# Router logits out of the shared expert's rest product, with the rests moved ahead of the router's choice and attention's statistics moved five half slots

## The chip, the core and the metric

The kernel runs on one core of one Trainium2 chip. The core has five engines with a queue each: TensorE (PE; its weight loads are shown as PEld), VectorE (DVE), ScalarE (ACT), GpSimd (POOL) and SyncE (SP, which here only issues DMAs). The metric is device time in microseconds (us): the median of three runs. Lower is better.

## What is computed

The reference is one cross-attention layer and one mixture-of-experts layer on 64 batches of 128 tokens with 128 features, all in float32. Cut to what matters:

```python
x = x + attention(layernorm(x), ctx)        # 16 heads of 64, 77 keys of 96 features per batch
x2 = layernorm(x)
logits = x2 @ router_w.T                    # 8 experts
scores = softmax(logits)
_, idx = top_k(scores, 2)                   # the two best experts of each token
rw = take_along_axis(logits, idx)           # weights are the logits themselves
moe = sum over e: gate[e] * (silu(x2 @ w1[e].T) * (x2 @ w3[e].T)) @ w2[e].T
shared = (silu(x2 @ sw1.T) * (x2 @ sw3.T)) @ sw2.T
x = x + moe + shared                        # inner width of each expert: 176
```

## The kernel before

**Groups, units and half slots.** Four batches make a group, and there are 16 groups (NG). A unit is one batch and 8 of its 16 heads, so a group has 8 units and the kernel 128. The main loop (L1099 to L1116) goes through the units. For unit k it emits, in this order: the scores of unit k + 2 (`scores`, L357), at every second unit the output product of the batch before (`out`, L439), the plan's steps of half slot 2k, the transposes of unit k's weights (`transposes`, L424), the exponentials of unit k + 2 (`exps`, L378), a value product (`values`, L401), the plan's steps of half slot 2k + 1, and the softmax weights of unit k + 2 (`weights`, L382). Everything else hangs in a plan (`at`, L858): a list of steps for each half slot. Group g starts at half slot p = 16 g.

**Order.** The last lines (L1121 to L1131) chain the instructions of each engine in the order in which they were emitted. So an engine works through its queue strictly as written, and a wait of one instruction holds all those behind it on that engine. Buffers are waited for by semaphores.

**Attention.** The query weights are folded into the keys' weights and the output weights into the values' weights. In each half slot PE makes keys for two heads (`keys`, pk, L348) and ACT copies them out (kx, L355). `scores` makes two products into the tile ps, which has one buffer of two PSUM banks (pool ps_s, L92 and L362); DVE takes the maximum (mx, L374) and subtracts it (sc, L376), and then ps is free for the next unit. ACT takes the exponential with the layer norm's factor rs as its scale (L380). DVE sums and inverts (sm, L387; ri, L389), and POOL multiplies (at, L395 to L399). PE transposes (pa, L434), ACT copies (aT, L437). Value products go from pv (L417) to vo by two ACT copies (L422). `out` sums ten products (py, L444), and DVE adds the residual (x1, L445). Six more PSUM banks (pool ps_g, `bank`, L234) serve all the rest. In odd groups four products of the last keys are added (`values_of_last`, pn L454, vn L462), each with an ACT copy and a DMA that ACT issues.

**Layer norm.** `Norm.stats` (L287) is four bn_stats, four bn_aggr and one addition on DVE and one power on POOL. Attention needs only its factor rs, in `exps`; its mean is folded away. The statistics for group g + 1 are taken in half slot p + 2 (L911). For the router, `scale` (L299) makes the normed tokens (pay, four ACT instructions), `transposed` (L313) makes x2T.

**Routing.** The router of group g runs while group g + 1 is in attention, p being that group's first half slot: statistics in p, normed in p + 1, transposed in p + 3, logits in p + 4, the first choice in p + 5, the second in p + 6 (L933 to L935). `logits` (L550) multiplies x2T by the router's weights rw_sb, batch by batch, into the tile pl; DVE copies it (lg, L557), takes the maximum (gm, L559) and subtracts it (gsc, L561), ACT takes the exponential (L562). `choose` (L574) sums (gs, L578), inverts, multiplies, clears what is too small, and finds the first maximum in five instructions (L564). `place` (p + 8) computes each token's row, and `send` (p + 9 to p + 12) scatters the tokens to DRAM, eight DMAs that POOL issues.

**Shared expert.** The inner width of 176 is split into 128 and a rest of 48 (IR). The weights lie packed in wsh_sb: columns 0 to 127 for w1, 128 to 255 for w3, then 112 columns (HI) for both rests, w1's in the first 48 and w3's in the last 48, with 16 columns between them left at zero. `shared_up` (p + 11) multiplies by the first two parts, `shared_rest` (p + 12) by the 112 columns (ph_s, L654), with tanh on ACT (ar_s, L518) and two instructions on DVE (ur_s, L520; hr, L521), `shared_down` (p + 14) by the second weights. The tile hr is one of NHR = 2 that are zeroed once and shared with the experts' blocks. The last three groups (LATE) run the shared expert in the ending.

**Experts.** Tokens are gathered in three sets of 9, 5 and 2 groups. When a set is full, blocks of its tokens go through the experts four at a time (`Quad`): from half slot 160, the start of group 10, the first set's 20 quads run beside attention, the others mostly in the ending (L1043), after attention. A quad loads tokens (xb), copies weights (w, on ACT and DVE), transposes (pt, xT L777), multiplies (p and ph, L782), and sends answers.

Of the kernel before, what the change touches and what calls it, by code (L numbers as in the profile page):

```python
# [27 lines left out]
IR = I - 128  # L28
HI = 64 + IR

W1, W3, WR, W2F, W2R, WALL = 0, 128, 256, 256 + HI, 384 + HI, 512 + HI
G = 4
NG = B // G

# [19 lines left out]

AHEAD = 2
NAT = 2
NHR = 2
NX1 = 3

# [7 lines left out]
def xattn_moe_kernel(  # L67
# [9 lines left out]
    wvT: bass.AP,  # L77
    w_out: bass.AP,
    b_out: bass.AP,
    rwT: bass.AP,  # L80
    wx: bass.AP,
    wsh: bass.AP,
    out: bass.AP,
# [69 lines left out]
    rw_sb = const.tile([D, E], F32, name="rw_sb")  # L153
    wsh_sb = const.tile([128, WALL], F32, name="wsh_sb")

    wx_sb = const.tile([128, E, WALL], F32, name="wx_sb")
    nc.scalar.dma_start(out=bo_sb, in_=b_out.rearrange("(o d) -> o d", o=1).broadcast_to([128, D]))
    nc.sync.dma_start(out=rw_sb, in_=rwT)
    nc.sync.dma_start(out=wsh_sb, in_=wsh)

    def load_expert(e):
# [28 lines left out]

    dest = const.tile([128, 2 * G], F32, name="dest")

    hrs = [const.tile([128, T], F32, name=f"hr_{i}") for i in range(NHR)]

    nobody = const.tile([128, DW], F32, name="nobody")

# [84 lines left out]
    class Norm:  # L281
# [3 lines left out]
            self.name, self.src = name, src  # L285

        def stats(self):  # L287
            st = small.tile([128, G, 6], F32, tag="st", name=f"st_{self.name}")
            self.mv = small.tile([128, G, 2], F32, tag="mv", name=f"mv_{self.name}")
# [4 lines left out]
            ve = small.tile([128, G], F32, tag="ve", name=f"ve_{self.name}")  # L294
            nc.vector.tensor_scalar(ve, self.mv[:, :, 1], EPS, None, ALU.add)
            self.rs = small.tile([128, G], F32, tag="rs", name=f"rs_{self.name}")
            nc.gpsimd.tensor_tensor(self.rs, ve, mhalf, ALU.pow)

        def scale(self, to):  # L299
# [186 lines left out]
    def gated(name, up, silu=False, n=T):  # L486

        p1 = bank(f"p1_{name}")
        up(p1, W1, 128)
        p3 = bank(f"p3_{name}")  # L490
        up(p3, W3, 128)
        a = ffn.tile([128, T], F32, tag="a", name=f"a_{name}")
        h = ffn.tile([128, T], F32, tag="h", name=f"h_{name}", bufs=3)
        of = slice(0, n)
        if silu:
            nc.scalar.activation(a[:, of], p1[:, of], AF.Silu)
            nc.vector.scalar_tensor_tensor(h[:, of], a[:, of], 2.0, p3[:, of], ALU.mult, ALU.mult)
# [8 lines left out]
    def gated_rest(name, up, silu=False, n=T):  # L506
# [4 lines left out]
        hr = hrs[hr_no[0] % NHR]  # L511
        hr_no[0] += 1
        of = slice(0, n)
        if silu:
            nc.scalar.activation(a[64:HI, of], pr[:IR, of], AF.Silu)
            nc.vector.scalar_tensor_tensor(hr[:IR, of], a[64:HI, of], 2.0, pr[64:HI, of], ALU.mult, ALU.mult)
        else:
            nc.scalar.activation(a[:IR, of], pr[:IR, of], AF.Tanh, scale=0.5)  # L518
            u = ffn.tile([128, T], F32, tag="u", name=f"ur_{name}")
            nc.vector.scalar_tensor_tensor(u[64:HI, of], a[:IR, of], 1.0, pr[:IR, of], ALU.add, ALU.mult)  # L520
            nc.vector.tensor_tensor(hr[:IR, of], u[64:HI, of], pr[64:HI, of], ALU.mult)  # L521
        return hr

    class Router:
# [23 lines left out]
            nc.scalar.copy(self.pay[:, 1, :, :D], self.pay[:, 0, :, :D])  # L548

        def logits(self):  # L550
            pl = bank(f"pl_{self.g}")
            for b in range(G):
                nc.tensor.matmul(
                    pl[:, b * E : (b + 1) * E], self.x2T[:, b * NQ : (b + 1) * NQ], rw_sb, start=True, stop=True
                )
            self.lg = lg = self.t3("lg")
            nc.vector.tensor_copy(lg.rearrange("p b e -> p (b e)"), pl[:, : G * E])  # L557
# [4 lines left out]
            nc.scalar.activation(sc, sc, AF.Exp)  # L562
# [32 lines left out]
        def place(self):  # L595
# [20 lines left out]
            )  # L616
            pos = small.tile([128, 2 * G], F32, tag="pos", name=f"pos_{g}", bufs=1)
            for src, to, by in ((at, pos, 1.0), (self.lg, self.pay[:, :, :, D + 1].rearrange("p c b -> p c b"), 0.5)):
                m = small.tile([128, 2, G, E], F32, tag="picked", name=f"picked_{g}", bufs=2)
                for k in range(2):  # L620
                    nc.vector.scalar_tensor_tensor(m[:, k], oh[:, k], by, src, ALU.mult, ALU.mult)
                if to is pos:
                    nc.vector.tensor_reduce(pos, m.rearrange("p c b e -> p (c b) e"), AX.X, ALU.add)
                else:
                    nc.vector.tensor_reduce(to, m, AX.X, ALU.add)
# [31 lines left out]
            self.h = gated(f"s{self.g}", self.up, silu)  # L657

        def shared_rest(self, silu=False):
            self.hr = gated_rest(f"s{self.g}", self.up, silu)  # L660

        def shared_down(self):
            py = bank(f"pf_{self.g}")
# [238 lines left out]
    for g in range(NG):  # L902
# [29 lines left out]
    assert g == NG  # L932
    for g in range(NG - 1):  # L933
        p = 16 * (g + 1)
        routing(g, p, (0, "stats"), (1, "normed"), (3, "transpose"), (4, "logits"), (5, "choose"), (6, "choose_second"))  # L935
    for st in sets:
        for g in range(st.start, min(st.start + st.n, NG - 1)):
            p = 16 * (g + 1)
            routing(g, p, (8, "place"))
            if g < NG - LATE:  # L940
                routing(g, p, (11, "shared_up"), (12, "shared_rest"), (14, "shared_down"), (17, "park"))
            for k in range(4):
                for c in range(2):
                    at(p + 9 + k, lambda g=g, c=c, b=k: routers[g].send(c, b))
# [189 lines left out]
def _laid_out(inputs):  # L1134
# [6 lines left out]
    def packed(w1, w3, w2):  # L1141
# [16 lines left out]
    def by_pair(w):  # L1158
# [15 lines left out]
        "rwT": a["L0_ffn_router_w"].T,  # L1174
        "wx": np.concatenate([packed(w1[e], w3[e], w2[e]) for e in range(E)]),
        "wsh": packed(a["L0_ffn_sw1"], a["L0_ffn_sw3"], a["L0_ffn_sw2"]),
    }


# [17 lines left out]
```

## Time and profile before

| what | us |
|---|---|
| median of three runs (lowest, highest) | 988.45 (987.61, 989.02) |
| the profiled execution | 985.48 |
| its span, first to last instruction | 983.8 |
| PE busy | 924.1 |
| DVE busy | 671.4 |
| ACT busy | 652.8 |
| POOL busy | 517.4 |
| mean granted TensorE clock | 0.978 of full |

The span has four stages. Until about 60 us the first group runs, after the weights are folded. From 60 to 466 us attention and routing of groups 1 to 9 run, without expert blocks. From 466 to about 830 us attention runs with the first set's quads beside it. The rest is the ending.

How to read the views: a row of the order of time shows start, length, engine, line, operation, the tile written and the tiles read; in brackets stands the idle time before it and what ended that. The chain of waits runs back from the last instruction, at each step to what released it. In a row of windows PEclk is the clock that TensorE was granted, 1.00 being full. A PE product's length includes its latency, so products overlap; the chain shows what each adds.

A float32 product takes two passes of weight load and matmul on PE, a transpose takes one: 640 transposes of L434 show 640 rows, 64 logits products of L553 show 128.

### The profile page before, as it was taken

The page shows a single profiled execution, that of the slowest core. Times are in us where ns is not written, and L with a number is a line of the kernel's source. Part 1 is how long each engine was busy: PE and PEld are TensorE (multiplying, and loading weights), DVE is VectorE, ACT ScalarE, POOL GpSimd, SP SyncE. Part 2 cuts the span into 40 slices and gives each one's busy share as a digit, 9 for nine tenths or more (in the row PEclk, how much of TensorE's full clock was granted, in tenths as well). Part 3 has the DMA queues.
Part 4 walks back from the last instruction along what each step waited for, and adds up shares of the span by engine and source line. Part 5 has one row for each costly group of instructions (what it writes and reads, how often), then busy time and mean ns, then how long its engine had stood idle before and what let it go on. Part 6 is the DMA issues. An engine that isn't in the chain of part 4 may idle for free.

```text
span 983.8 us, 18867 instructions
## 1 busy us (share of the span) xinstructions
PE 924.1 (94%) x6123; PEld 771.5 (78%) x6123; DVE 671.4 (68%) x1751; ACT 652.8 (66%) x1420; POOL 517.4 (53%) x688
## 2 busy tenths in 40 slices
PE   8999999999999999999999999999999987779990
PEld 7887877787787878777888788888888876678980
DVE  4566776676667767768687677776676779566642
ACT  5776767676767667675776767667767665556760
POOL 3244563636364544636367375574474564437673
PEclk9999999999999999999999999999999999879996
DMA  6222212212222222122322221223121135723475
GB/s 179 70 62 71 67 41 81 68 57 71 72 71 65 75 73 65 44 86 80 89 70 76 83 82 55 59 69 99 57 85 49 37 121 169 228 66 98 109 212 174
DMA packets 80882, 85.76 MB, mean 87 GB/s; under 512 B 11328, under 2 KB 62912, under 8 KB 80784
## 3 DMA queue, kind: packets, MB, share of 16 engines
q1 hardware_dynamic: 65920, 56.09, 20.8%
q0 software_dynamic: 8864, 18.30, 5.6%
q10 hardware_dynamic: 6000, 10.16, 2.9%
q8 instruction: 49, 0.80, 0.3%
q14 instruction: 49, 0.40, 0.1%
HBM read 48.18 MB, written 36.33 MB: 86 GB/s over the span
## 4 chain that ended last, share of the span: by engine, by line
PE 69%; DVE 10%; ACT 9%; DMA 5%; issue 4%; SPq 2%; POOL 1%; ACTq 0%; DVEq 0%; POOLq 0%
PE py L444 13%; PE ps L365 11%; PE pk L348 11%; PE pv L417 8%; PE pa L434 5%; PE p L782 4%; PE p_s L654 3%; PE pn L454 2%; PE ph L782 2%; PE pq L794 2%; PE pq L795 2%; DMA answers<-y,to 2%; PE pf L667 1%; PE pf L666 1%; DMA out_dram<-yx 1%
## 5 line engine op out<-in xcount | busy, mean ns | idle before, releaser
L348 PEld LDWEIGHTS pk<-cT,wkq_sb 96*128 96x128 f32 x1024 | 157.8, 189 | 70.0 <-issue 42.8
L805 POOL DMA_INDIRECT answers<-y,to x149 | 146.4, 983 | 89.7 <-issue 44.7
L355 ACT COPY kx<-pk 128x308 f32<-128x308 f32 x256 | 104.5, 417 | 128.5 <-PE pk L348 123.2
L348 PE MATMUL pk<-cT,wkq_sb 96*128 96x154 f32 x1024 | 175.0, 294 | 1.0 <-ACT wkq_sb L265 0.7
L444 PEld LDWEIGHTS py<-vo,aT 128*128 128x128 f32 x1280 | 155.7, 194 | 15.8 <-ACT vo L422 5.2
L365 PE MATMUL ps<-kx,xgT 128*128 128x308 f32 x512 | 156.8, 426 | 9.7 <-DVE sc L376 9.1
L444 PE MATMUL py<-vo,aT 128*128 128x128 f32 x1280 | 157.9, 278 | 4.3 <-ACT vo L422 3.9
L643 POOL DMA_INDIRECT sent<-pay,row x128 | 126.3, 987 | 61.5 <-DVE part L633 27.6
L397 POOL TENSOR_TENSOR at<-sc,ri 128x512 f32<-128x512 f32 x64 | 67.2, 1050 | 170.9 <-DVE ri L389 117.6
L422 ACT COPY vo<-pv 64x512 f32<-64x512 f32 x256 | 147.3, 575 | 2.1 <-ACT vn L462 0.4
L417 PE MATMUL pv<-wvo_sb,cM 96*128 96x512 f32 x256 | 131.1, 594 | 1.0 <-DVE hr L521 0.8
L387 DVE TENSOR_REDUCE sm<-sc 128x8 f32<-128x616 f32 x128 | 101.1, 790 | 39.6 <-ACT sc L380 38.8
L380 ACT ACTIVATE sc<-sc,rs_a 128x616 f32<-128x616 f32 x128 | 105.0, 820 | 26.9 <-DVE sc L376 17.9
L365 PEld LDWEIGHTS ps<-kx,xgT 128*128 128x128 f32 x512 | 88.9, 189 | 38.6 <-issue 9.4
L437 ACT COPY aT<-pa 128x512 f32<-128x512 f32 (+1 forms) x256 | 96.2, 430 | 33.9 <-PE pa L434 29.2
L395 POOL TENSOR_TENSOR at<-sc,ri 128x256 f32<-128x256 f32 x128 | 77.1, 625 | 79.1 <-DVE ri L389 25.3
L376 DVE TENSOR_TENSOR sc<-ps,mx 128x616 f32<-128x616 f32 x128 | 102.4, 800 | 12.5 <-POOL at L399 0.4
L374 DVE TENSOR_REDUCE mx<-ps 128x8 f32<-128x616 f32 x128 | 98.3, 768 | 7.6 <-PE ps L365 6.4
L434 PE MATMUL pa<-ident,at 128*128 128x128 f32 x640 | 92.2, 275 | 0.0
L782 PE MATMUL p<-xT,w 128*128 128x128 f32 x596 | 77.0, 284 | 10.8 <-ACT xT L777 5.5
L434 PEld LDWEIGHTS pa<-ident,at 128*128 128x128 f32 x640 | 75.7, 143 | 11.2 <-issue 10.7
L782 PEld LDWEIGHTS p<-xT,w 128*128 128x128 f32 x596 | 72.8, 198 | 14.6 <-ACT xT L777 8.0
(152 smaller groups left out, 1405.6 us busy)
## 6 DMA issues: line engine op xcount, KB each, us to landing
xb<-sent SPq DMA_DIRECT2D x149, 65.0 KB
last_values<-vn ACTq DMA_DIRECT2D x32, 256.0 KB
vo<-last_values SPq DMA_DIRECT2D x64, 128.0 KB
ya<-answers SPq DMA_DIRECT2D x15, 512.0 KB
xgT<-in_xT_dram SPq DMA_DIRECT2D x16, 256.0 KB
xg<-in_x_dram SPq DMA_DIRECT2D x16, 256.0 KB
parked<-x SPq DMA_DIRECT2D x14, 256.0 KB
yx<-parked SPq DMA_DIRECT2D x14, 256.0 KB
```

What stands on the lines that cost most here:

```text
L348: nc.tensor.matmul(pk[:, k].rearrange("p (b k) -> p b k", k=NKV), wkq_sb[:, 2 * i + k, :], self.cT[:, 2 * p : 2 * (p + 1), :], start=True, ...
L355: nc.scalar.copy(self.kx[p][:, hs, :], pk)
L365: nc.tensor.matmul(ps[:, r, : 4 * NKV].rearrange("p (j k) -> p j k", k=NKV), self.xgT[:, ts], self.kx[p][:, h : h + 4, ks], start=True, st ...
L376: nc.vector.tensor_tensor(at, sc, over_keys(mx), ALU.subtract)
L380: nc.scalar.activation(at, at, AF.Exp, scale=self.norm.rs[:, b : b + 1])
L417: nc.tensor.matmul(pv, self.cM[:, p, KM * r : KM * (r + 2)], wvo_sb[:, h : h + 4, :], start=True, stop=True)
L422: nc.scalar.copy(self.vo[b][rows, 4 * t : 4 * (t + 1), :], pv[rows].rearrange("p (m d) -> p m d", d=D))
L434: nc.tensor.transpose(pa[:, j * NQ : (j + 1) * NQ], keys[:, c : c + 128], ident)
L444: nc.tensor.matmul(py[:, :D], aT[:, m, :], vo[:, m, :], start=(m == 0), stop=(m == NT - 1))
L643: ins = nc.gpsimd.indirect_dma_start(out=sent[st.i], out_offset=bass.IndirectOffsetOnAxis(ap=self.row[:, i : i + 1], axis=0), in_=self.pay ...
L782: nc.tensor.matmul(to[:m, ts], self.w[j][:, c : c + m], self.xT[:, ts], start=True, stop=True)
L805: ins = nc.gpsimd.indirect_dma_start(out=answers[st.i], out_offset=bass.IndirectOffsetOnAxis(ap=self.to[:, j : j + 1], axis=0), in_=self.y ...
```

## The change

Three things change, and buffers are rearranged for them.

1. The router's weights (8 columns) are written into the unused columns between the two rests, at WG = WR + 48. The rests' product, still 112 columns wide, then holds the logits, transposed, in rows 48 to 55. `shared_rest` moves from half slot p + 12 to p + 4 for the routers of groups 0 to 12. Before its tanh, ACT copies all 112 rows to the tile lT. In half slot p + 5 `logits_of_rest` transposes lT batch by batch (four transposes), and DVE reads the eight columns as the logits. What follows (`weigh`) is the old code: lg, gm, gsc and the exponential. The routers of groups 13 to 15 keep a product of their own, with the weights taken from wsh_sb.
2. The logits are now in half slot p + 5, and the first choice stays there, directly behind them.
3. Attention's statistics for group g + 1 are emitted in half slot p - 3 instead of p + 2 (for g = 0 still in 2).

The buffers: hr of the shared expert gets a third tile of its own, since it now lives from p + 4 to p + 14; h has 2 buffers instead of 3, picked 1 instead of 2, the statistics' tiles 4 instead of 3; lT takes one of the two buffers of the tag u. The router's own weight tile and its DMA go.

```diff
+WG = WR + IR
...
-    nc.sync.dma_start(out=rw_sb, in_=rwT)
...
-    hrs = [const.tile([128, T], F32, name=f"hr_{i}") for i in range(NHR)]
+    hrs = [const.tile([128, T], F32, name=f"hr_{i}") for i in range(NHR + 1)]
...
-        h = ffn.tile([128, T], F32, tag="h", name=f"h_{name}", bufs=3)
+        h = ffn.tile([128, T], F32, tag="h", name=f"h_{name}", bufs=2)
...
         def logits(self):
-            pl = bank(f"pl_{self.g}")
+
+            pl = bank(f"pl_{self.g}")[:, : G * E].rearrange("p (b e) -> p b e", e=E)
             for b in range(G):
                 nc.tensor.matmul(
-                    pl[:, b * E : (b + 1) * E], self.x2T[:, b * NQ : (b + 1) * NQ], rw_sb, start=True, stop=True
+                    pl[:, b, :], self.x2T[:, b * NQ : (b + 1) * NQ], wsh_sb[:, WG : WG + E], start=True, stop=True
                 )
+            self.weigh(pl)
+
+        def logits_of_rest(self):
+
+            pl = bank(f"pl_{self.g}").rearrange("p (b e) -> p b e", b=G)
+            for b in range(G):
+                nc.tensor.transpose(pl[:, b, :HI], self.lT[:HI, b * NQ : (b + 1) * NQ], ident[:HI, :HI])
+            self.weigh(pl[:, :, IR : IR + E])
+
+        def weigh(self, pl):
             self.lg = lg = self.t3("lg")
-            nc.vector.tensor_copy(lg.rearrange("p b e -> p (b e)"), pl[:, : G * E])
+            nc.vector.tensor_copy(lg, pl)
...
-                m = small.tile([128, 2, G, E], F32, tag="picked", name=f"picked_{g}", bufs=2)
+                m = small.tile([128, 2, G, E], F32, tag="picked", name=f"picked_{g}", bufs=1)
...
         def shared_rest(self, silu=False):
-            self.hr = gated_rest(f"s{self.g}", self.up, silu)
+            def up(to, c, m):
+                self.up(to, c, m)
+                if not silu:
+                    self.lT = ffn.tile([128, T], F32, tag="u", name=f"lT_{self.g}")
+                    nc.scalar.copy(self.lT[:HI], to[:HI])
+
+            self.hr = gated_rest(f"s{self.g}", up, silu, hr=None if silu else hrs[NHR])
...
-            at(p + 2, lambda g=g: stats(g + 1))
+            at(p - 3 if g else 2, lambda g=g: stats(g + 1))
...
-        routing(g, p, (0, "stats"), (1, "normed"), (3, "transpose"), (4, "logits"), (5, "choose"), (6, "choose_second"))
+        routing(g, p, (0, "stats"), (1, "normed"), (3, "transpose"))
+        if g < NG - LATE:
+            routing(g, p, (4, "shared_rest"), (5, "logits_of_rest"))
+        else:
+            routing(g, p, (4, "logits"))
+        routing(g, p, (5, "choose"), (6, "choose_second"))
...
-                routing(g, p, (11, "shared_up"), (12, "shared_rest"), (14, "shared_down"), (17, "park"))
+                routing(g, p, (11, "shared_up"), (14, "shared_down"), (17, "park"))
...
+    shared = packed(a["L0_ffn_sw1"], a["L0_ffn_sw3"], a["L0_ffn_sw2"])
+    shared[:, WG : WG + E] = a["L0_ffn_router_w"].T
```

More of the change, by code (lines that the diff above doesn't have):

```diff
@@ L79, in xattn_moe_kernel @@
     b_out: bass.AP,
-    rwT: bass.AP,
     wx: bass.AP,
@@ L152, in xattn_moe_kernel @@
     bo_sb = const.tile([128, D], F32, name="bo_sb")
-    rw_sb = const.tile([D, E], F32, name="rw_sb")
     wsh_sb = const.tile([128, WALL], F32, name="wsh_sb")
@@ L287, in stats @@
         def stats(self):
-            st = small.tile([128, G, 6], F32, tag="st", name=f"st_{self.name}")
-            self.mv = small.tile([128, G, 2], F32, tag="mv", name=f"mv_{self.name}")
+            st = small.tile([128, G, 6], F32, tag="st", name=f"st_{self.name}", bufs=4)
+            self.mv = small.tile([128, G, 2], F32, tag="mv", name=f"mv_{self.name}", bufs=4)
             for b in range(G):
@@ L293, in stats @@
                 nc.vector.bn_aggr(self.mv[:, b, :], st[:, b, :])
-            ve = small.tile([128, G], F32, tag="ve", name=f"ve_{self.name}")
+            ve = small.tile([128, G], F32, tag="ve", name=f"ve_{self.name}", bufs=4)
             nc.vector.tensor_scalar(ve, self.mv[:, :, 1], EPS, None, ALU.add)
-            self.rs = small.tile([128, G], F32, tag="rs", name=f"rs_{self.name}")
+            self.rs = small.tile([128, G], F32, tag="rs", name=f"rs_{self.name}", bufs=4)
             nc.gpsimd.tensor_tensor(self.rs, ve, mhalf, ALU.pow)
@@ L504, in gated, with gated_rest @@
         return h
-    def gated_rest(name, up, silu=False, n=T):
+    def gated_rest(name, up, silu=False, n=T, hr=None):
         pr = bank(f"ph_{name}")
@@ L510, in gated_rest @@
         a = ffn.tile([128, T], F32, tag="a", name=f"ar_{name}")
-        hr = hrs[hr_no[0] % NHR]
-        hr_no[0] += 1
+        if hr is None:
+            hr = hrs[hr_no[0] % NHR]
+            hr_no[0] += 1
         of = slice(0, n)
@@ L1173, in _laid_out @@
         "b_out": a["L0_xattn_b_out"],
-        "rwT": a["L0_ffn_router_w"].T,
         "wx": np.concatenate([packed(w1[e], w3[e], w2[e]) for e in range(E)]),
-        "wsh": packed(a["L0_ffn_sw1"], a["L0_ffn_sw3"], a["L0_ffn_sw2"]),
+        "wsh": shared,
     }
```

## The prediction

> **What bounds the kernel now.** I read the page first, then the windows by stage, the chain of waits over one group, and DVE, ACT and POOL in order of time in that group. The profiled execution took 985.48 us, its span 983.8, 1.68 lie around it. The median of the three timed runs is 988.45, 2.97 above. I sum changes against the span and add them to the median.
>
> ```profile
> span 983.8 us, 18867 instructions
> ...
> PE 924.1 (94%) x6123; PEld 771.5 (78%) x6123; DVE 671.4 (68%) x1751; ACT 652.8 (66%) x1420; POOL 517.4 (53%) x688
> ```
>
> The windows (columns: stretch, length, then busy time of PE, PEld, DVE, ACT, POOL, then the granted clock) show that PE is the bound until the blocks join at 466 us:
>
> ```profile
> 60.50:465.80 405.30, 402.90 (x2461) 320.45 (x2461) 290.09 (x821) 280.56 (x603) 204.79 (x277) 1.00 0.23 68
> ```
>
> PE is idle 2.4 us in 405 there. So PE work taken out is a gain, and any new PE wait is a loss at full price. DVE's 290 of 405 is an average; what matters is one place. The chain of waits leaves PE once per even group, at the router's choice (start, length, what):
>
> ```profile
> 300.48 0.81 PE pl L553 x8
> ...
> 301.31 0.20 DVE lg L557
> ...
> 301.98 0.24 ACT gsc L562
> ...
> 302.25 0.20 DVE gs L578
> ...
> 304.03 0.19 DVE oh L572
> 304.22 0.72 DVE sm L387
> ...
> 305.16 0.68 DVE mx L374
> ...
> 305.93 0.80 DVE sc L376
> ...
> 306.88 1.28 PE ps L365 x4
> ```
>
> The scores have one PSUM buffer (L362), so PE's scores of unit k+4 wait until DVE has read those of unit k+3 (sc L376), and that DVE work is queued behind the first choice. Today this wait is 0.35 us in an even group (row "PE ps <- DVE sc") and nothing in an odd one, where products of the last keys give PE more to do. **DVE has no room after the choice begins.** All hangs on when the choice's first instruction (gs) can start: 302.25 now.
>
> **The parts.** The changed routing runs for routers 0 to 12, in attention groups 1 to 13.
>
> (1) Logits. Eight passes (pl, 0.81 us) go; four transposes of 112 columns come. The nearest row is x2's transpose, four of 128 columns in 0.44 us (296.05 in the chain); a transpose is one pass, a product two (640 rows of L434 for 640 transposes, 128 of L553 for 64 products). PE saves 0.81 - 0.44 = 0.37 us a group, 4.8 us in thirteen. The router's weights ride in unused columns of the rests' product, which stays 112 wide: nothing.
>
> (2) Rests moved from half slot 12 to 4: PE 0.86 us (ph_s x2), ACT's ar_s, DVE's ur_s and hr. The same work, but in front of the choice.
>
> (3) New copy lT on ACT, 112x512 out of PSUM. That shape has no row; x2T's 128x512 copy takes 0.59 and lets the next one start after 0.48. Bounds 0.42 (the 128x308 copy) and 0.60; I take 0.59, the same columns.
>
> (4) The exponential of the logits. It was issued in half slot 4, ahead of ACT's work for the unit. Now it is issued in half slot 5, behind these:
>
> ```profile
> 302.12 0.74 ACT L437 COPY aT<-pa 128x512 f32<-128x512 f32 x2
> 302.74 0.82 ACT L380 ACTIVATE sc<-sc,rs_a 128x616 f32<-128x616 f32 x1
> 303.45 1.18 ACT L422 COPY vo<-pv 64x512 f32<-64x512 f32 x2
> 304.65 0.73 ACT L355 COPY kx<-pk 128x308 f32<-128x308 f32 x2
> ```
>
> Starts are 0.62, 0.71 and 1.20 apart, a kx takes 0.31 to the next start. And DVE's choice, its next instruction, waits for that exponential.
>
> Now the slot again, on this group's times, even group. PE: pk ends 300.48, rests 301.34, aT's transposes 301.9, pv 302.76, pk 303.28, logits 303.72. ACT: lT 301.37, ar_s 301.85 to 302.44, aT 302.33, exp 302.95, vo 303.66, kx 304.86, router's exponential 305.17 to 305.40. DVE: free at 300.28 (after x L445), waits 2.2 us for ar_s; ur_s 302.47, hr 303.19, lg 303.91 (0.72 apart, as at 323.56 and 324.28), gm, gsc to 304.55; waits 0.85 us; gs at 305.42 instead of 302.25: **3.17 us later**. From there the chain is the same, so sc ends 309.90 instead of 306.73 and PE's scores start at 310.05 instead of 306.88. PE alone would have been there at 306.88 - 0.35 + 0.86 - 0.37 = 307.02: a wait of 3.0. At half slot 12 PE then saves the 0.86. Net 3.17 - 0.86 = +2.31 us. Queued behind DVE's wait are sm and ri, so POOL's weights; they are needed only after the next output product (2.23 us), so that is covered.
>
> Odd group (340.50): PE's rests end 345.64 + 0.86 = 346.50; ACT has vn and its DMA issue until 346.62; lT 346.64, ar_s 347.12, aT 347.60, exp 348.22, vo 348.93, kx 350.13, exponential 350.44 to 350.67; gs 350.69 instead of 347.40, 3.29 later. Scores at 355.32 instead of 352.62 (no wait before; 353.11 natural): +2.70, less 0.86, is +1.84, with a wait of 2.2.
>
> Groups 1 to 9 (five odd, four even): 5 x 1.84 + 4 x 2.31 = **+18.4 us**, the 0.37 in it.
>
> (5) Groups 10 to 13, with expert blocks. DVE is late there for other reasons and ACT idles 1.4 to 2.8 us waiting for the router's gsc (2.78 at 623.73), which now lies behind work that it can do meanwhile. By the same steps: +0.7 at 482 us (gs 2 us later, scores at 501.1 instead of 499.56, less 0.86). In the three others xT, which ACT runs behind gsc, comes 0.3 to 0.8 sooner and takes PE's waits at p with it (0.34 at 566.06, 0.53 at 629.10, 0.65 of the 1.00 at 697.84), while PE has 0.86 - 0.37 more to do before and 0.86 less after: -0.7, -0.9 and -1.0. Together -1.9. Bounds: -3.7 (4 x 0.37 and all these waits with the 0.35 at 626.02), and +8.3 if all four behave like groups 1 to 9 (4 x 2.08, their mean). I take -1.9.
>
> (6) Statistics 5 half slots sooner. DVE 1.34 us (295.35 to 296.69) leave a place where DVE waits for ACT's exp until 297.27 anyway: no gain. They arrive where ur_s and hr (1.4) have left. POOL's power (1.01) comes between the sends; the weights behind it then end near 329.2 and PE takes them at about 333: covered; without that cover 1.0 a group. One late wait of PE (0.92 at 768.69) shrinks by some 0.5: -0.5.
>
> (7) Fewer buffers for h and picked, one more hr, no router DMA: h is rewritten only after down products that stand earlier in PE's own order, picked lives on DVE alone, hr's memset (0.52) is POOL's at the start. Nothing; if covers fail, DVE waits of tenths.
>
> (8) **The clock.** PE's granted clock fell to half for whole stretches of 3.41 us here:
>
> ```profile
> 820.82:824.24 3.42, 1.21 (x5) 0.77 (x5) 3.28 (x5) 2.00 (x5) 3.04 (x4) 1.00 0.63 208
> 824.24:827.65 3.41, 3.41 (x17) 3.23 (x16) 3.15 (x10) 0.85 (x2) 1.28 (x2) 0.50 0.27 101
> ...
> 749.15:752.56 3.41, 1.87 (x11) 1.20 (x10) 3.24 (x8) 0.79 (x4) 1.50 (x3) 1.00 0.00 0
> 752.56:755.97 3.41, 3.41 (x25) 3.11 (x26) 3.28 (x14) 3.37 (x7) 2.08 (x3) 1.00 0.00 0
> ```
>
> A stretch with 1.21 us of PE work (one idle gap of 2.21, the same scores wait) was followed by half clock; one with 1.87 was not. So it takes between 1.55 and 2.2 idle us in one stretch; I take 1.87. A gap of about 2.95 (even) puts that much into one stretch in (1.54 + 1.07) / 3.41 = 77% of positions, one of 2.1 (odd) in some 52%: 4 x 0.77 + 5 x 0.52 = 5.7 stretches. Each costs up to half of 3.41 = 1.7, less where the gap runs into it: 1.4 on average, +8. Bounds 0 and 9 x 1.7 = 15.3.
>
> [...]
>
> **Sum:** +18.4 - 1.9 - 0.5 + 8 = +24.0. 985.5 + 24.0 = 1009.5 for a profiled run, 988.45 + 24.0 = 1012.4 for the median; I say **1012**.
>
> **Rivals.** (A) Forecast: a scores wait of 2 to 3 us in each of groups 1 to 9, half clock behind about half of them. 62%, 1007 to 1020. (B) The waits without the clock: 988.45 + 16.0 = 1004.4. For it: the odd gaps lie near the limit. 18%. (C) The groups with blocks stall too: +8.3 instead of -1.9 is 10.2 more, 1022.7. For it: DVE gets more to do there as well. 13%. (D) The other side, faster: DVE's queue hides all. That needs gs at 302.4 or sooner (307.02 less the 4.6 from gs to PE's scores): the exponential would have to overtake exp, vo and kx on ACT and the rests' work be done by then. Then only PE's saving counts: 988.45 - 4.8 - 0.5 = 983.1. Against it: ACT's rows run strictly in program order, L1121 to L1131 pin that order, and ur_s alone can't start before 302.47. That the emitted order is not the one I read belongs here. 5%. Left, 2%, for no change, a half-way house.
>
> Range: from B with the blocks at their best (1004.4 - 1.8, and the waits shorter by a tenth of a us each) to C with a few more slow stretches: 1001 to 1026; I leave out 2 in 10. About 0.2% (2 us) is what a measurement can tell from no change. Faster 0.05, same 0.02, slower 0.93.
>
> **What shows it.** In the new profile: pl in one pass, four rows a router (else step 1 fails); "DVE gs <- ACT gsc" near 0.85 us a group; "PE ps <- DVE sc" some 13 waits of 2 to 3 us instead of 7, together over 20 us; PE's clock below 1.00 between 60 and 466 us; the shared product's wait at half slot 12 gone; the span from 60 to 466 longer by 18 to 30 us and that of the blocks equal within 5. I am wrong if DVE reaches the choice within half a us of before, or if PE's idle time in the middle stays near 2.4 us.

## The result and the profile after

The changed kernel takes **1016.08 us** (median of 6 runs, 1013.99 to 1016.83), the kernel before 988.19 beside it (6 runs, 986.41 to 989.02): ratio 1.0282, 95% interval 1.0269 to 1.0295. The forecast was 1012, the range 1001 to 1026. The profiled execution took 1016.2 us.

The page's head, to be held against the two lines of before:

```profile
span 1014.5 us, 18788 instructions
...
PE 928.5 (92%) x6071; PEld 772.8 (76%) x6071; DVE 687.7 (68%) x1751; ACT 659.9 (65%) x1433; POOL 518.6 (51%) x689
```

PE has 52 instructions fewer, four a router, and yet is busy 4.4 us longer: it ran slower for a while. The first windows of after show where the time went (columns as in the prediction; the last two are the DMA engines' share and GB/s):

```profile
60.50:466.00 405.50, 385.04 (x2298) 305.41 (x2298) 277.49 (x756) 271.46 (x582) 187.80 (x257) 0.98 0.21 62
```

In the same 405 us PE now does 2298 instructions instead of 2461, and it idles 20.5 us instead of 2.4. I cut both traces at the start of each group (the start of the scores of its third unit, since scores run two units ahead):

| stage | before | after | difference |
|---|---|---|---|
| groups 1, 3, 5, 7, each | 46.5 | 48.5 | +1.95 |
| groups 2, 4, 6, 8, each | 43.3 | 47.3 | +4.0 |
| group 9 | 48.91 | 53.61 | +4.70 |
| groups 10 to 13 (blocks), together | 267.44 | 266.86 | -0.58 |
| groups 14, 15 and what follows | 247.6 | 250.2 | +2.6 |

(4 x 1.95 + 4 x 4.0 + 4.70 - 0.58 + 2.6 and 0.2 before group 1 make the 30.7 between the spans.) The medians differ by 27.9 only: the traced execution of before, 985.48 us, was quicker than all six timed runs beside it, while that of after lay at its median. A second trace of the changed kernel agrees in each of groups 1 to 13 to 0.15 us, so those 2.8 us most likely belong to the last row. So the loss sits in groups 1 to 9, and the view of waits names it (us in all, times, longest):

```profile
PE ps L364 <- DVE grest L601: 22.5, 9, 2.9
PE ps L364 <- DVE sc L375: 11.4, 9, 2.5
DVE gs L589 <- ACT gsc L573: 10.5, 13, 1.2
```

The scores wait 18 times for DVE, where they waited 7 times and 9.1 us before, and the choice (gs) waits for the exponential in each of the thirteen routers. (grest is the tiny DVE instruction directly behind the subtraction sc, and ends just before the scores start; what frees ps is sc.) The same place in the even group that the prediction worked out, first DVE, then ACT, then PE in order of time:

```profile
314.07 0.29 DVE L444 TENSOR_TENSOR x<-py,x 128x128 f32<-128x128 f32 x1
316.56 0.68 DVE L520 SCALAR_TENSOR_TENSOR ur_s<-ar_s,ph_s 48x512 f32<-48x512 f32 x1 [2.20 <-ACT ar_s L518]
317.27 0.69 DVE L521 TENSOR_TENSOR hr<-ur_s,ph_s 48x512 f32<-48x512 f32 x1
318.00 0.19 DVE L568 COPY lg<-pl 128x32 f32<-128x32 f32 x1
...
318.44 0.19 DVE L572 TENSOR_TENSOR gsc<-lg,gm 128x32 f32<-128x32 f32 x1
319.54 0.19 DVE L589 TENSOR_REDUCE gs<-gsc 128x4 f32<-128x32 f32 x1 [0.91 <-ACT gsc L573]
...
323.22 0.80 DVE L375 TENSOR_TENSOR sc<-ps,mx 128x616 f32<-128x616 f32 x1
```
```profile
315.46 0.58 ACT L675 COPY lT<-ph_s 112x512 f32<-112x512 f32 x1 [0.45 <-PE ph_s L665]
315.94 0.59 ACT L518 ACTIVATE ar_s<-ph_s 48x512 f32<-48x512 f32 x1
...
317.76 1.18 ACT L421 COPY vo<-pv 64x512 f32<-64x512 f32 x2
318.96 0.42 ACT L354 COPY kx<-pk 128x308 f32<-128x308 f32 x1
319.28 0.23 ACT L573 ACTIVATE gsc<-gsc 128x32 f32<-128x32 f32 x1
```
```profile
317.19 0.55 PE L563 MATMUL pl<-ident,lT 112*128 112x112 f32 x4
...
324.17 2.19 PE L364 MATMUL ps<-kx,xgT 128*128 128x308 f32 x4 [2.91 <-DVE grest L601]
```

DVE idles twice, 2.20 us for ar_s and 0.91 us for the exponential, and both gaps stand in front of the choice. The exponential is the last of ACT's queue: lT, ar_s, vo and kx all go first, though its input (gsc) is there at 318.63. Against the start of the unit's scores (310.41 here, 296.33 before) the choice begins at 9.13 instead of 5.92 us. Of these 3.2 us, 2.6 are there already when DVE takes up the logits (lg, 7.59 instead of 4.98): PE makes them half a slot later, behind the rests' product, and DVE does ur_s and hr first. The exponential adds 0.6, a wait of 0.91 instead of 0.30. The same two DVE rows before:

```profile
301.31 0.19 DVE L557 COPY lg<-pl 128x32 f32<-128x32 f32 x1 [1.03 <-PE pl L553]
...
302.25 0.19 DVE L578 TENSOR_REDUCE gs<-gsc 128x4 f32<-128x32 f32 x1 [0.30 <-ACT gsc L562]
```

In the change the next subtraction (sc) stands at 323.22, PE's scores then start after 2.91 us of idle time, and their length, 2.19 instead of 1.28, shows the half clock:

```profile
320.97:324.38 3.41, 0.50 (x4) 0.30 (x3) 3.13 (x10) 0.00 (x0) 1.39 (x2) 1.00 0.00 0
324.38:327.79 3.41, 3.41 (x12) 2.71 (x12) 3.13 (x9) 2.27 (x4) 1.22 (x2) 0.50 0.01 2
...
368.75:372.16 3.41, 2.53 (x13) 1.52 (x11) 3.04 (x12) 1.68 (x5) 0.26 (x1) 1.00 0.20 77
372.16:375.58 3.42, 2.13 (x14) 1.87 (x15) 3.08 (x11) 2.21 (x4) 1.12 (x2) 1.00 0.00 0
375.58:378.99 3.41, 3.41 (x30) 2.84 (x29) 2.23 (x7) 1.06 (x3) 1.39 (x2) 1.00 0.02 5
```

The first two are the even group: 0.50 us of PE work in a stretch of 3.41, then a stretch at half clock. The other three lie around the odd group's wait of 2.17 us. On the same grid of stretches (13 further on) it falls into two of them, which keep 2.53 and 2.13 us of work, and the clock stays.

### The profile page after: what moved, and what is told of

The parts are those of the page before. It is cut to its first block, busy times and chain, and to the rows that moved or that the text cites. A ratio compares the mean times of both kernels' runs of the same rounds, so it can differ in the third digit from the quotient of the medians.

```text
span 1014.5 us, 18788 instructions
## 1 busy us (share of the span) xinstructions
PE 928.5 (92%) x6071; PEld 772.8 (76%) x6071; DVE 687.7 (68%) x1751; ACT 659.9 (65%) x1433; POOL 518.6 (51%) x689
## 3 DMA queue, kind: packets, MB, share of 16 engines
q1 hardware_dynamic: 65776, 56.09, 20.5%
## 4 chain that ended last, share of the span: by engine, by line
PE 63%; DVE 14%; ACT 11%; DMA 6%; issue 3%; SPq 1%; ACTq 1%; DVEq 0%; POOL 0%; POOLq 0%
PE py L443 13%; PE ps L364 11%; PE pk L347 10%; PE pv L416 7%; PE pa L433 4%; PE p L799 4%; DMA answers<-y,to 3%; PE p_s L665 3%; PE pn L453 2%; DVE sc L375 2%; DVE sm L386 2%; ACT vo L421 2%; PE pq L811 2%; DVE mx L373 2%; PE pq L812 2%
## 5 line engine op out<-in xcount | busy, mean ns | idle before, releaser
L364 PE MATMUL ps<-kx,xgT 128*128 128x308 f32 x512 | 160.5, 435 | 34.0 <-DVE grest L601 22.5
L443 PEld LDWEIGHTS py<-vo,aT 128*128 128x128 f32 x1280 | 157.9, 196 | 16.8 <-ACT vo L421 5.4
```

What stands on the lines that cost most here:

```text
L364: nc.tensor.matmul(ps[:, r, : 4 * NKV].rearrange("p (j k) -> p j k", k=NKV), self.xgT[:, ts], self.kx[p][:, h : h + 4, ks], start=True, st ...
L443: nc.tensor.matmul(py[:, :D], aT[:, m, :], vo[:, m, :], start=(m == 0), stop=(m == NT - 1))
```

## The experiments

Each edit is against the changed kernel. **My theory:** the change puts ACT's queue and the rests' DVE work in front of the choice, so the scores wait (some 2.2 us an odd group, 3 an even one), and the clock falls behind the longest of these waits. **Rivals:** the statistics at their new place, the rests alone without the exponential's place in the queue, or a chip that ran slower, which has nothing to do with the waits.

The first four kernels ran together on a chip where the kernel before takes 1036.94 us (16 runs, 1032.69 to 1041.41). One kernel, the one with the statistics back, was traced there and on a faster chip: its groups 1 to 9 last the same on both (to 0.05 us), and only the groups with blocks (291.5 us instead of 267.1) and what follows (286.2 instead of 250.3) are longer. Ratios are against that time, and group times carry the verdicts. The other eight ran on two chips where the kernel before takes 988.50 (985.98 to 990.62, 23 runs) and 987.19 (985.85 to 990.70, 23 runs).

**The statistics back at their old place, alone.**

```diff
-            at(p - 3 if g else 2, lambda g=g: stats(g + 1))
+            at(p + 2, lambda g=g: stats(g + 1))
```

> The changed kernel with attention's statistics back in half slot p + 2; all else changed. Theory (the choice starts some 3 us late because the rests' work and ACT's exponential stand ahead of it; the statistics lie where DVE waits for ACT either way): within 1.5 us of the changed kernel, 1015 to 1018, the same five half-clock stretches or so. Rival (the statistics in their new place push DVE's work in front of the scores): at least 5 us faster than the changed kernel, 1011 or less. Second rival (they are what keeps the change from being worse): 5 us or more slower, since 1.34 us of DVE come back in each of 14 groups.

Measured: 1075.52, ratio 1.0370 (1.0344 to 1.0396). Groups 1 to 9 are those of the changed kernel to 0.05 us. The statistics are no part of the loss there; while the waits at the choice are there, their place is worth nothing either way in these groups. From group 10 on this kernel is 13 to 14 us longer than the next three on that chip, which keep the statistics early; the changed kernel itself did not run there, so how much the place moves in the groups with blocks this chip could not tell, and the kernel was run again (below).

**The choice in the logits' half slot, but the rests where they were.** The logits keep a product of their own, issued in half slot 5 directly before the choice; no lT.

```diff
-            routing(g, p, (4, "shared_rest"), (5, "logits_of_rest"))
+            routing(g, p, (5, "logits"))
...
-                routing(g, p, (11, "shared_up"), (14, "shared_down"), (17, "park"))
+                routing(g, p, (11, "shared_up"), (12, "shared_rest"), (14, "shared_down"), (17, "park"))
```

> The changed kernel without two of its parts: the rests stay in half slot 12 and the logits are a product of their own, but that product stands in half slot 5, directly ahead of the choice. So only the exponential's place on ACT, behind the unit's copies, is changed. Theory: the choice's sum waits for the exponential until about 1.95 us later than before; scores 1.95 us later in an even group and 1.43 in an odd one, 4 x 1.95 + 5 x 1.43 = 15 us in groups 1 to 9, up to 6 more where the even groups' gap of 2.3 us brings the half clock, 0 to 4 from the groups with blocks: 1003 to 1013. Rival (the rests' work ahead of the choice is the only cause): 987 to 991.

Measured: 1057.93, ratio 1.0209 (1.0182 to 1.0236); odd groups 48.37, most even groups 46.88 (45.25 in the one without a half-clock stretch), group 9 51.7. This part alone makes nearly all of the odd groups' loss (48.47 in the full change). But two things move in it: the exponential goes behind ACT's work for the unit, and PE makes the logits half a slot later. The rows that tell them apart stand with the last experiment.

**The rests early, but the logits and the choice as before** (and no lT).

```diff
-            routing(g, p, (4, "shared_rest"), (5, "logits_of_rest"))
...
+        routing(g, p, (4, "logits"))
+        if g < NG - LATE:
+            routing(g, p, (4, "shared_rest"))
```

> The changed kernel with the rests in half slot 4, but behind a logits product of the router's own in the same half slot, without the copy lT and without the transposes: the exponential keeps its early place on ACT. So only the rests' work ahead of the choice is changed. Theory: the choice starts about 2.0 us later in an even group (1.85 odd); PE has 0.86 more to do before it, so scores shift by 2.0 less 0.86 = +1.14 even, +0.4 odd, net: 6.6 us in groups 1 to 9, gaps of 1.5 us at most, so no half clock; -1 to +4 from the groups with blocks: 994 to 999. Rival (the exponential's place on ACT is the only cause): 987 to 990.

Measured: 1047.27, ratio 1.0123 (1.0088 to 1.0158), so 10.3 us on that chip. Odd groups +0.86, even +1.38, group 9 +4.8. The direction was right, the size at the upper edge, above all through group 9, which I had counted as an odd group and which has two half-clock stretches (from 472.75), where I expected none. The two halves are not additive: +1.85 and +0.86 in an odd group make +1.95 together. In the full change the rests' DVE work (2 x 0.7) lies inside the time in which DVE would wait for the logits anyway (2.96 us in an even group of the kernel with the choice in the same half slot).

**Both choices one half slot later.** The logits and the exponential then have a half slot to come round.

```diff
-            routing(g, p, (4, "shared_rest"), (5, "logits_of_rest"))
+            routing(g, p, (4, "shared_rest"), (5, "logits_of_rest"), (6, "choose"), (7, "choose_second"))
```

> The changed kernel with the first choice in half slot 6 and the second in 7 (routers 0 to 12); all else changed. The DVE work of the two units is the same, only its order differs: DVE sums, maximizes and subtracts for the scores before the choice. Theory (the wait for the exponential and the choice's place in front of the scores cost, not the amount of DVE work): scores waits of 0.2 to 0.3 us in an even group and none in an odd one, no half clock between 60 and 480 us, PE's 0.37 us a group kept: 9 x 0.35 = 3 us faster than before in groups 1 to 9, the groups with blocks -2 to +3: 982 to 988. Rival (DVE has too much to do in these two units in any order): waits of 1 to 2 us stay, 997 or more.

Measured: 1042.44, ratio 1.0051 (1.0030 to 1.0072). Odd groups 46.14, -0.38 against before, so PE's saving appears; even groups 43.88, +0.55. The long wait is gone and with it the half clock in groups 1 to 8. Group 9 takes 52.34 (+3.4), with two half-clock stretches from 463.79, which I had not expected. And two waits stand in an even group:

```profile
324.83 1.28 PE L364 MATMUL ps<-kx,xgT 128*128 128x308 f32 x4 [0.28 <-issue]
...
330.75 1.28 PE L364 MATMUL ps<-kx,xgT 128*128 128x308 f32 x4 [0.40 <-DVE sc L375]
```

By the starts of the rows they delay the scores by 0.45 and 0.56 us (keys to scores 0.97 and 1.08 apart, 0.52 where nothing waits; two expectations further down have 0.53, 0.54 and 0.64 for such waits). So the 3 us of gain did not come. The second wait was new to me. DVE, then POOL, of this kernel in order of time:

```profile
325.97 2.13 DVE L294 TENSOR_SCALAR ve_a<-mv_a 128x4 f32<-128x4 f32 x1
```
```profile
325.32 1.19 POOL L394 TENSOR_TENSOR at<-sc,ri 128x256 f32<-128x256 f32 x2
326.47 0.38 POOL L398 TENSOR_TENSOR at<-sc,ri 128x104 f32<-128x104 f32 x1
326.80 1.26 POOL L336 TENSOR_TENSOR x<-xg,bo_sb 128x512 f32<-128x512 f32 x1
```

The statistics' last DVE instruction, an addition on 128x4 elements, takes 2.13 us. It ends at 328.10, just after POOL's long addition (328.06). All of DVE's queue stands behind it, the maximum and the subtraction for the scores included.

**The changed kernel again, and with the gap filled.** The second kernel issues 16 transposes of the identity in half slot p + 7 of groups 1 to 9, where PE waits. They take one turn of the six shared banks, and nobody reads what they write. They add some 1.75 us of PE work a group (16 x 0.11, by the row of four transposes in 0.44).

```diff
+    def fill(n):
+        pi = bank("fill")
+        for _ in range(n):
+            nc.tensor.transpose(pi[:, :128], ident, ident)
+
+    for g in range(9):
+        at(16 * (g + 1) + 7, lambda: fill(16))
```

> The changed kernel itself, on the chip of this set of runs, so that the others can be read against it. Groups 1 to 9 by the trace as in its first profile: 48.47 us in odd groups, 47.3 in even ones. If the loss is PE's own schedule, the same 27 to 29 us over the kernel before; if expert blocks and ending answer to the chip (memory, DMAs), another difference there.

> The changed kernel with 16 transposes of the identity (some 1.75 us of PE work that nobody reads) as the last step of half slot p + 7 in groups 1 to 9, just ahead of the scores that wait. Theory (an idle gap in one stretch of 3.41 us brings the half clock, and that costs PE time): the work fits into the waits of 2.4 and 3.2 us, the gaps left are 0.7 and 1.4 us, no half clock between 60 and 480 us; even groups 47.3 - 1.65 = 45.7 us, odd ones unchanged at 48.5; in all some 6 us faster than the changed kernel, with more work. Rival (the lower clock costs nothing, because PE waits for DVE anyway): no gain, 0 to +2. Second rival (PE was not idle there): 9 x 1.75 = 16 us slower.

Measured: 1015.88, ratio 1.0291 (1.0264 to 1.0318), and 1010.45, ratio 1.0217 (1.0199 to 1.0236). **More PE work, 5.4 us less time.** PE of the filled kernel in order of time, and its groups 1 to 8 as a window:

```profile
317.25 1.91 PE L278 MATMUL fill<-ident 128*128 128x128 f32 x16
...
320.33 1.29 PE L370 MATMUL ps<-kx,xgT 128*128 128x308 f32 x4 [1.17 <-DVE grest L607]
```
```profile
60.70:419.00 358.30, 352.14 (x2191) 282.60 (x2191) 250.62 (x687) 242.17 (x519) 167.77 (x230) 1.00 0.21 62
```

The scores take 1.29 again instead of 2.19, the mean clock is 1.00, and an even group lasts 45.68 instead of 47.32. So the clock's share is 1.64 us an even group, caused by PE's idle stretch, and the waits' own share is 45.68 - 43.32 = 2.36. Group 9 keeps its half-clock stretch (at 482.80) and 53.39 us: the fill does not stand in front of the wait behind the routing's tables.

**Choices later and statistics back.** The kernel above with later choices, with the first experiment's edit added.

```diff
-            at(p - 3 if g else 2, lambda g=g: stats(g + 1))
+            at(p + 2, lambda g=g: stats(g + 1))
...
-            routing(g, p, (4, "shared_rest"), (5, "logits_of_rest"))
+            routing(g, p, (4, "shared_rest"), (5, "logits_of_rest"), (6, "choose"), (7, "choose_second"))
```

> The kernel with the choices in half slots 6 and 7, and attention's statistics back in p + 2. In that kernel's trace the statistics' small addition on DVE took 2.0 to 2.1 us instead of 0.17 in groups 1 to 8, beside POOL's residual addition, and PE's scores waited 0.54 and 0.64 us behind it in even groups. Theory (that collision is what the even groups lost): the addition back at 0.17, even groups 43.9 to about 43.1 us, odd ones unchanged at 46.1; 3 us faster than that kernel. Rival (DVE has too much work around there anyway): even groups stay at 43.9.

Measured: 987.81 against 988.50, ratio 0.9995 (0.9985 to 1.0005): no difference from the kernel before. The 28 us of loss are gone. (Group 9 takes 49.57: its wait is 2.51 us, but no stretch holds more than 1.75 of it, and the clock stays.) The view by line shows the addition (shortest, median, longest ns; then first and last start) in the later-choices kernel and in this one:

```profile
L294 DVE TENSOR_SCALAR ve_a<-mv_a x16: 170/1093/2134, 9.7 to 750.3; 128x4 f32<-128x4 f32 x16
```
```profile
L294 DVE TENSOR_SCALAR ve_a<-mv_a x16: 170/170/287, 9.5 to 751.3; 128x4 f32<-128x4 f32 x16
```

With the statistics at their old place it is back at 0.17 us, and even groups go from 43.87 to 43.32. That equals before, though PE's products are 0.43 us shorter: a wait takes it back. DVE, ACT and PE at that wait:

```profile
319.76 0.69 DVE L501 SCALAR_TENSOR_TENSOR u_s<-a_s,p_s 128x512 f32<-128x512 f32 x1 [2.93 <-ACT a_s L499]
```
```profile
317.63 1.15 ACT L421 COPY vo<-pv 64x512 f32<-64x512 f32 x2
...
319.12 0.60 ACT L499 ACTIVATE a_s<-p_s 128x512 f32<-128x512 f32 x1
```
```profile
323.89 1.29 PE L364 MATMUL ps<-kx,xgT 128*128 128x308 f32 x4 [0.28 <-DVE sc L375]
```

At the shared expert's first product DVE waits for the tanh a_s, which stands behind vo in ACT's queue, as the exponential does in the change. The rests used to give PE 0.86 us to do in the half slot behind; now they have left, and the scores are reached before DVE is done.

**That order for routers 0 to 7 only** (the edits above under `g < 8`, the old order for the others, the statistics back for all).

> As e7_later_stats_back, but only for the routers of groups 0 to 7; the others keep the order of before (a logits product of their own in half slot 4, rests in 12, choices in 5 and 6). Theory: groups 1 to 8 take 46.1 and 43.1 us instead of 46.5 and 43.3, 2 to 3 us less in all, group 9 (with the tables) 48.9 as before, blocks and ending as before: 2 to 3 us faster than the kernel before. Rival (what PE saves in the groups comes back as a wait further on): 0.

Measured: 988.41, ratio 0.9999 (0.9989 to 1.0010): the 2 to 3 us did not come, as the rival had it. Groups 1 to 8 are 1.4 shorter together, -0.45 in each odd one and a little back in the even ones. Group 9, with the old order, lost 1.9 of it: its wait behind the routing's tables, 1.65 us as in before, now had a half-clock stretch behind it (at 462.11). The ending took 2.7 more, but this trace is of an execution of 988.99 and that of before of one of 985.48, so this can be run against run.

**The shared product one half slot later** (the kernel with later choices and the statistics back, and `(12, "shared_up")` for `(11, "shared_up")`).

> As e7_later_stats_back (choices in 6 and 7, statistics in p + 2), and the shared expert's first products in half slot 12 instead of 11, in the place that the rests left. In e7's trace DVE's u_s waits 2.9 us in every even group for a_s, which ACT runs behind the unit's value copies, and PE's scores wait 0.53 us at the next unit but one, since PE has 0.86 us less to do there. Theory (the 0.86 taken from half slot 12 uncovers this chain): that wait goes, even groups 43.3 to 42.8 or 42.9 us, odd ones unchanged at 46.1, group 9 (tables) -1 to +1; 984.5 to 987, some 2 us faster than e7 and 2 to 4 faster than before. Rival (another wait takes its place): even groups stay at 43.3, 988.

Measured: 989.06, ratio 1.0015 (1.0001 to 1.0029). Another wait took the place of the first, as the rival had it, and a longer one: even groups got 0.48 longer, not shorter. Without p_s in half slot 11 the scores before it are reached too early, as PE shows:

```profile
317.48 1.28 PE L364 MATMUL ps<-kx,xgT 128*128 128x308 f32 x4 [0.77 <-PE pk L347]
```

The row names pk as the last releaser by the profile; pk had run long before in PE's own order, so what ended the gap was the buffer ps: DVE's subtraction for the unit before ends at 317.38. PE work that is moved away from in front of the scores opens a wait wherever DVE is just in time.

**The change for routers 9 to 12 only**, which run beside the expert blocks (`9 <= g < NG - LATE`; statistics as in the change).

> The changed kernel, but with the change's order only for the routers of groups 9 to 12, which run beside expert blocks; routers 0 to 8 keep logits in half slot 4 and rests in 12. Statistics in p - 3 everywhere. Theory (the loss is groups 1 to 9 alone): these take 46.5 and 43.3 us as before, the groups with blocks 64.3, 68.9, 64.6 and 69.0 as in the changed kernel (-0.6 together), so 986 to 989. Rival (the groups with blocks or the ending carry part of the loss): 991 or more.

Measured: 989.64, ratio 1.0015 (1.0004 to 1.0027). The groups with blocks are those of the changed kernel (64.32, 68.89, 64.63, 69.00), some 0.6 us less together than before, so there the change does no harm. Group 9 got 2.1 longer, by a half-clock stretch at 463.50. So the median lies between the theory's 989 and the rival's 991. The traced execution, 991.32, was the longest of twelve and has a longer ending too, which says little.

**Two of the first set on a faster chip:** the statistics back, and the choice in the logits' half slot with the rests late (the edits as shown above).

> The changed kernel with attention's statistics back in half slot p + 2 once more, since e1 was timed on a chip on which the kernel before took 1037 us. Theory: the changed kernel's 1016 within 1.5 us. Rival: more than 3 us off it, either way.

> e2 once more (rests in half slot 12, a logits product of its own, directly ahead of the choice in half slot 5), since e2 too was timed on the slower chip. By e2's trace odd groups take 1.86 us more than before and even ones 3.57 (one without the half clock 1.93), group 9 2.8 more: 20 to 24 us over the kernel before, if blocks and ending add nothing: 1008 to 1012. Rival (the blocks add as well): 1014 or more.

Measured: 1018.46, ratio 1.0319 (1.0300 to 1.0337), and 1011.10, ratio 1.0231 (1.0212 to 1.0251). The first is 2.4 above the changed kernel, and some 3.7 by the ratios (1.0319 against 1.0282): more than I had allowed. Groups 1 to 9 are the same to 0.05 us. Its traced execution was its quickest, 1016.28, and as long as that of the change, so where the difference lies is not shown.

The second is 5 us below the changed kernel. In its profile the exponential starts 7.58 us after its unit (318.28 - 310.70), against 8.87 in the change (319.28 - 310.41) and 5.65 before, and the scores wait 1.99 us instead of 2.91. What the choice waits for there, by DVE's rows of an even group:

```profile
317.61 0.19 DVE L568 COPY lg<-pl 128x32 f32<-128x32 f32 x1 [2.96 <-PE pl L554]
...
318.55 0.18 DVE L589 TENSOR_REDUCE gs<-gsc 128x4 f32<-128x32 f32 x1 [0.30 <-ACT gsc L573]
```

DVE idles 2.96 us for the logits, and then 0.30 for the exponential, no longer than before. (In odd groups the second wait is 0.73 instead of 0.30.) My expectation had taken the exponential's place on ACT for the only thing changed; what costs here is mostly that PE makes the logits half a slot later, directly in front of the choice. That alone costs 24 us of the 28, with five half-clock stretches in groups 1 to 8, and the early rests, lT and the exponential's longer wait add the rest. No run moves the exponential's place alone.

## Why the prediction was right

By its own steps, measured against predicted:

- **Logits.** Four rows a router, 0.38 us against 0.44 assumed (317.19 to 317.57): PE saves 0.43 to 0.46 a group. The odd groups of the kernel with later choices and old statistics keep it, 46.07 against 46.52.
- **lT and the exponential on ACT.** The copy takes 0.58 and lets the next start after 0.48 (315.46, 315.94), as assumed. lg starts 7.59 us after its unit's start (310.41), gs 9.13; the sum gave 7.58 and 9.09. So the path to the choice was right step by step, the 0.85 of wait for the exponential (0.91) included. Most of the delay lies ahead of that wait, in the later logits and in the rests' work on DVE.
- **Scores.** They start 13.76 us after the unit's start, predicted 13.72. Even groups +2.36 without the clock, predicted 2.31; odd +1.95, predicted 1.84, with a wait of 2.17 at 373.44, predicted 2.2. The wait of before, 0.35 in the sum, stands in no row; by the starts of PE's rows it is 0.27 (keys at 306.08, scores at 306.88, 0.53 apart where nothing waits).
- **Group 9** was taken as an odd group, +1.84; it lost 4.70. This is the term that was most in error. The rests' 0.86 us that leave half slot 12 are not given back there, because DVE's work on the tables holds the scores (a wait of 2.51 at 490.42 instead of 1.65 at 463.32 before), and a half-clock stretch follows (491.63).
- **The clock.** Predicted 5.7 stretches and 8 us; there are 5 in groups 1 to 9 (133.23, 228.81, 324.38, 419.95, 491.63), at 1.64 each (measured in the even groups) 8.2 us. The sum was right, the reason only in part, so its closeness is partly luck: I treated positions as chance and gave odd gaps a half share. The stretches hit all four even groups and, of the five counted as odd, only group 9 (the last section). A gap of 2.91 us with 0.50 us of work in the stretch was enough, and so were 2.20 us idle before 491.63.
- **Groups with blocks.** +0.68, -0.35, -1.28 and +0.37, together -0.58; predicted +0.7, -0.7, -0.9 and -1.0, together -1.9. Group 13 was wrong. Groups 14 and 15 gave +0.3 in place of the -0.5 put down for the statistics.
- **Statistics.** No gain and no loss in groups 1 to 9, as predicted. In the whole the kernel with them back was 2.4 us slower, more than the 0.5 put down, and where is not shown. What I missed is that the addition stretches to 1.63 us in the median; it lies in the shadow of the other waits and shows only once these are gone.
- **The ending** was put at nothing and took 2.3 more in the trace; the half-clock stretches fall elsewhere in it. I did not separate that further. Since the traced execution of before was 2.7 us quicker than its median, this can be run against run.
- **The sum.** Predicted +24.0; +27.9 by the medians, within the range. What was too small in it: the waits by 0.6, group 9 by 1.2 beyond its share as an odd group and its clock stretch, the groups with blocks by 1.3, groups 14 and 15 by 0.8.

## What to carry to other kernels

When a step is moved within half a slot, write out the queue of every engine that it crosses; here a choice kept in its half slot, while its logits came 2.6 us later and its exponential of 0.23 us another 0.6, made the bounding engine wait 2 to 3 us a group, and moving the choice on by half a slot took these waits away. Removing 0.4 us of work from the bounding engine is worth nothing where the next buffer is handed over just in time: ask first what it would wait for. And price a wait on TensorE above its length: in the changed kernel, where its idle time filled 2.20 us or more of a stretch of 3.41, the next stretch was at half clock each time (the scores took 2.19 us instead of 1.28).

## What the runs showed of the hardware

**The clock's stretches run nearly in step with the loop.** In the trace of the changed kernel every drop to half clock begins a whole number of stretches of 3.413 us behind the first, at 133.23 (491.63 is 105 of them on, 904.64 is 226). A pair of groups lasts 95.8 us there, and 28 stretches are 95.57. So the same gap falls on nearly the same part of a stretch each time: 133.23, 228.81, 324.38 and 419.95 are 95.57 apart, one in each even group, and the odd groups' gap is cut in two by the grid each time. I laid that grid over the traces of before and after, from 50 us on, and took PE's idle time in each stretch at full clock. With 2.20 us idle or more (eleven stretches) the next one was at half clock each time; with less than 1.42 it never was. Between lie both kinds: 1.42, 1.59 and 1.91 with a drop (the next stretch at 875.44 of before, 904.64 of after, 858.37 of before), and 1.54 and 1.96 without one (752.56 of before, 853.44 of after); so also 1.58 with a drop, in the stretch from 81.74 of the choice in the same half slot, run again, and 1.75 without one, in that from 461.08 of the kernel with later choices and old statistics. So no sharp limit is shown; the ends of PE's work are modelled in the profile, which blurs it.

**A tiny DVE instruction took 2 us beside POOL's work.** In the kernel with later choices the 128x4 addition goes from 0.17 to 2.13 us while POOL works through three instructions back to back (325.32 to 328.06), and ends 0.04 us after POOL's last. In groups 1 to 8 of that kernel it takes 2.0 to 2.1 us; in groups 1 to 8 of the changed one 1.63 to 1.81, ending 0.03 to 0.04 us behind POOL's long addition each time. In the same groups of the kernel before, no POOL instruction runs beside it, and it takes 0.17. What holds it was not shown.

**Chips differ in some stages only.** The kernel before took 988 us on one chip and 1037 on another. The kernel with the statistics back, traced on two such chips, took 1018 and 1076, its groups 1 to 9 equal to 0.05 us; the groups with expert blocks and what follows them made the difference. Why was not tried.
